# Twelve of 98 edge groups take their source rows from TensorE instead of gathers

## The chip, the cores and the metric

The kernel runs on one core of a Trainium2 chip. The metric is the device time of one execution in microseconds (us), the median of several. A core has TensorE (PE, matrix products into PSUM), VectorE (DVE), ScalarE (ACT), GpSimd (POOL, which issues the gathers here) and SyncE (SP, which issues the other transfers). Each works through its own list of instructions in order and waits on semaphores.

## The reference

One layer of a graph network over N = 6250 nodes and E = 100000 edges, with H = 128 features and 4 attributes per edge. Edges are sorted by destination. All data are float32.

```python
msg_in = concatenate([x[src], x[dst], edge_features], axis=1)
h = silu(msg_in @ mW1 + mb1)
messages = h @ mW2 + mb2
aggregated = segment_sum(messages, dst, num_segments=N)
u = silu(concatenate([x, aggregated], axis=1) @ uW1 + ub1)
out = layer_norm(x + layer_norm(x + u @ uW2 + ub2, ln_g, ln_b))
```

The last line is shortened: the inner norm is that of the layer, and the outer adds the input once more, without gain and bias.

## The kernel before

The first product is split by its rows: A = x @ mW1[:128] and B = x @ mW1[128:256] + mb1 are made once per node and stored in DRAM as tab_a and tab_b. An edge then needs A[src] + B[dst] + (attributes @ the last four rows).

Edges are worked in 98 groups of 1024 (eight tiles of 128 edges; the last group has six). Because edges are sorted by destination, a group touches a window of at most 80 successive nodes. For each group g:

- fetch (L181): POOL issues eight indirect transfers, each of which gathers 128 rows of A for the 128 sources of a tile, into a buffer "ga". There are six such buffers, and fetch runs four groups ahead in program order.
- load: SP brings the destinations (near), the 80 rows of B (mv) and the attributes (st, lower rows), three groups ahead.
- matrices: DVE compares, and so makes the 0/1 matrix st (L468: node by edge, with the count of edges per node) and its turned form oh (L478: edge by node), two groups ahead.
- before_rows (L500): eight products st x mv give B[dst] plus the attributes' part in PSUM (pre), one group ahead.
- hidden: DVE adds pre to the gathered rows (L515), ACT applies silu (L516) and so makes h.
- sums (L524): eight products h x oh, accumulated in PSUM (pt), sum h over the edges of each node. A small product (L522) turns the edge counts.
- add (L545): DVE adds the sums into an accumulator acc at an offset held in a register, and likewise the counts.

The order in which these calls stand in the loop is the order on each engine; there is no other scheduler:

```python
        load(g + LEAD)
        hidden(g)
        matrices(g + 2)
        if g + 1 >= RAW:
            before_rows(g + 1)
        add(g, sums(g))
        node_stage(g)
```

The first five groups (RAW) are gathered from x itself while tab_a is being made. PE turns their rows (L489) and multiplies them by the weights (L502). Nodes are finished in batches of four tiles of 128 nodes, one batch about every eight groups. When a batch closes, node_stage runs node_u in that group (products L562, L569, L570, silu, and the B rows of a later batch by L328), node_y in the next (products, then means and variances on DVE) and node_z in the one after (ACT scales, DVE multiplies, adds, and takes moments). Once at the end a flag (bad_i, from checks) tells whether the destinations fit the windows; if not, a general branch does everything again.

Of the kernel before, what the change touches and what calls it, by code (L numbers as in the profile page):

```python
# [1 line left out]

# [7 lines left out]
I32 = mybir.dt.int32  # L10
BF16 = mybir.dt.bfloat16
AF = mybir.ActivationFunctionType
# [6 lines left out]
P = 128  # L19
# [5 lines left out]
def kernel(  # L25
# [24 lines left out]
    G = 8  # L50
# [27 lines left out]
    assert rest_t == 5 and last[NB - 3] == NG - 10  # L78

    consts = ctx.enter_context(tc.tile_pool(name="consts", bufs=1))  # L80
    dram = ctx.enter_context(tc.tile_pool(name="dram", bufs=1, space=DRAM))
# [15 lines left out]
    edges = ExitStack()  # L97
    edges.enter_context(tc.manual_schedule())
    gath = edges.enter_context(tc.tile_pool(name="gath", bufs=AHEAD + 2))
    work = edges.enter_context(tc.tile_pool(name="edge", bufs=2))  # L100
# [9 lines left out]
    def narrow():  # L110
        return ps1.tile([P, 2 * P], F32, name="pt")

    def bank():
        return ps1.tile([P, BN, P], F32, name="pn")

    src_l = first.tile([SQ, SK, P], I32, name="src_l")
    nf_e = E // P
# [33 lines left out]
    nc.gpsimd.iota(w_row_i, pattern=[[1, W]], base=0, channel_multiplier=0)  # L151
    p_col_i = first.tile([P, 1], I32, name="p_col_i")
    nc.gpsimd.iota(p_col_i, pattern=[[0, 1]], base=0, channel_multiplier=1)

# [16 lines left out]
    tab_a = dram.tile([NP, H], F32, name="tab_a")  # L171
    tab_b = dram.tile([NW, H], F32, name="tab_b")
    ea_d = dram.tile([ED, NG * GE], F32, name="ea_d")
    rows, bases, near = {}, {}, {}
# [13 lines left out]
    for g in range(RAW - 1):  # L188
# [7 lines left out]
        ceil_i, pattern=[[BN * P, NB + 1], [0, G]], base=BN * P - W, channel_multiplier=0  # L196
    )
    fetch(RAW - 1)

# [16 lines left out]
    dst_l = dst_l[:NG]  # L216
    w_row = ps1.tile([P, W], F32, name="w_row")
    nc.vector.tensor_copy(w_row, w_row_i)
    p_col = consts.tile([P, 1], F32, name="p_col")
    nc.vector.tensor_copy(p_col, p_col_i)  # L220
    ones = consts.tile([P, P], F32, name="ones")
# [10 lines left out]
    off_i = consts.tile([1, NG], I32, name="off_i")  # L232
    bad_i = consts.tile([1, 1], I32, name="bad_i")

    def to_row(col, n):
# [4 lines left out]
    def destination_lists():  # L240
        base_c = first.tile([NG, 1], F32, name="base_c")
        nc.vector.tensor_copy(base_c, dst_l[:, 0:1])
        rel_n = first.tile([P, GE], F32, name="rel_n")[:NG]
        nc.vector.tensor_scalar(rel_n, dst_l, base_c, None, op0=OP.subtract)
        pt = wide()
        for i in range(G):
            nc.tensor.transpose(pt[:, i, :NG], rel_n[:, i * P : (i + 1) * P], ident[:NG, :NG])
        nc.vector.tensor_copy(rel.rearrange("c g i -> c i g"), pt[:, :, :NG])
        base_f = first.tile([1, NG], F32, name="base_f")
        row = to_row(base_c, NG)  # L250
        nc.vector.tensor_copy(base_f, row)
        p_b = narrow()
        nc.tensor.matmul(p_b[:, :NG], ones[0:1, :], base_f, start=True, stop=True)
        nc.vector.tensor_scalar(base_p, p_b[:, :NG], p_col, None, op0=OP.add)
        nc.vector.memset(floor_i[:, 0:1], 0)
        nc.vector.memset(floor_i[:, last[NB - 2] + 1 :], batches[NB - 1][0] * P)
        off = first.tile([1, NG], F32, name="off")
        nc.vector.tensor_copy(off, floor_i)
        nc.vector.tensor_sub(off, base_f, off)
        nc.vector.tensor_scalar(off_i, off, 0.0, float(AW - W), op0=OP.max, op1=OP.min)  # L260
        nc.vector.memset(ceil_i[:, 84 + G // 2 :], batches[NB - 1][0] * P - W)
        nc.vector.memset(ceil_i[:, 92 + G // 2 :], NP)
        lim = first.tile([1, NG], F32, name="lim")
        nc.vector.tensor_copy(lim, ceil_i[:, G // 2 : G // 2 + NG])
        nc.vector.tensor_tensor(base_i, base_f, lim, op=OP.min)
        return rel_n, base_f, off, lim

    def checks(rel_n, base_f, off, lim):
        far = first.tile([NG, 2], F32, name="far")
# [5 lines left out]
        nc.vector.tensor_reduce(far[:, 0:1], far, AX.X, OP.max)  # L275
        worst = first.tile([1, 4], F32, name="worst")
        nc.vector.tensor_reduce(worst[:, 0:1], to_row(far[:, 0:1], NG), AX.X, OP.max)
# [62 lines left out]
    def make_a(k, pm):  # L340
        i0, n = batches[k]
        product(k, 0, pm)
        ta = first.tile([P, BN, H], F32, name="ta", bufs=3)
        nc.vector.tensor_copy(ta[:, :n], pm[:, :n])  # L344
        nc.sync.dma_start(by_node(tab_a)[:, i0 : i0 + n, :], ta[:, :n])

# [92 lines left out]
    offs = {}  # L439

    def load_bases(g):
        for to, of, eng, top in ((bases, base_i, ENG.SP, NP), (offs, off_i, ENG.DVE, AW - W)):
# [10 lines left out]
    def load(g):  # L453
        if g >= NG:
            return
        destinations(g)
        if g % RB == 0:
            load_bases(g)
        nc.sync.dma_start(mv[g % NM][:W], tab_b[bass.ds(bases[g], W), :])
        nc.sync.dma_start(stbuf[g % NST][W:], ea_d[:, g * GE : (g + 1) * GE])  # L460

    oh, pre, xg = {}, {}, {}

    def matrices(g):
        if g >= NG:
            return
        n = tiles_of(g)
        nc.vector.tensor_scalar(  # L468
            stbuf[g % NST][:W],
            near.pop(g),  # L470
# [22 lines left out]
    def before_rows(g):  # L493
# [3 lines left out]
        pre[g] = wide()  # L497
        st = stbuf[g % NST].rearrange("k (i c) -> k i c", i=G)
        for i in range(tiles_of(g)):
            nc.tensor.matmul(pre[g][:, i, :], st[:, i, :], mv[g % NM], start=True, stop=not raw)  # L500
            if raw:
                nc.tensor.matmul(  # L502
                    pre[g][:, i, :], xg[g][:, i, :], w1[:, 0, :], start=False, stop=True
                )
        xg.pop(g, None)

    def hidden(g):
        n = tiles_of(g)
        h = hbuf[g % 2]
        p = pre.pop(g)  # L510
# [7 lines left out]
    def sums(g):  # L518
        n = tiles_of(g)
        h, o = hbuf[g % 2], oh.pop(g)  # L520
        pt = narrow()
# [105 lines left out]
    def node_stage(g):  # L627
# [10 lines left out]
        for k in range(2, NB):  # L638
# [4 lines left out]
            if g == G * k - G:  # L643
                make_b(k)

    open_batch(0)
    for g in range(2):
        load(g)
        matrices(g)
    load(2)  # L650
    turned_rows(0)
    for g in range(NG):
        if g == 2:
# [3 lines left out]
        if g == 6:  # L657
            checks(*lists)
            source_lists(1, SK)
            start.close()  # L660
        for c in range(1, NC):
            if g == max(1, c * EC // GE - 8):
                attributes(c)
            if g == max(1, c * EC // GE - 8) + 1:
                attribute_rows(c)
        if g + AHEAD >= RAW:
            fetch(g + AHEAD)
        if g < RAW:
            if g + 1 < RAW:
                turned_rows(g + 1)  # L670
            before_rows(g)
        load(g + LEAD)
        hidden(g)
        matrices(g + 2)
        if g + 1 >= RAW:
            before_rows(g + 1)
        if g == NG - 1:
            node_x(NB - 1)
        add(g, sums(g))
        node_stage(g)  # L680
    k = NB - 1
# [271 lines left out]
```

## Time and profile before

| what | value |
|---|---|
| median of 3 timed executions | 1033.82 us (1021.22 to 1034.26) |
| the profiled execution | 1463.32 us, its span 1461.5 us |
| TensorE's mean granted clock in it | 0.561 of full speed |
| TensorE busy | 885.3 us (61%) |
| VectorE busy | 451.3 us (31%) |
| ScalarE busy | 238.8 us (16%) |
| GpSimd busy | 739.3 us (51%) |
| gathers from tab_a | 742, mean 943 ns |
| gathers from x | 40, mean 947 ns |

In the groups and timelines of the profile a line reads: start in us, busy time in us, engine, source line, operation, what it writes <- what it reads, shape, number of instructions, and in brackets the idle time of the engine just before, with what ended it. In the list of waits a line reads: who waited <- for whom, total us, times, longest. PEclk is the granted TensorE clock in tenths of full speed, in 40 slices of the span. A float32 product of 128x128 by up to 512 columns appears as two MATMUL instructions and two weight loads (PEld). "Remote" stands for a wait whose end the profile can put down to nothing on this core. The profiled execution took longer than the timed ones; the prediction deals with that.

### The profile page before, as it was taken

The page shows a single profiled execution, that of the slowest core. Times are in us where ns is not written, and L with a number is a line of the kernel's source. Part 1 is how long each engine was busy: PE and PEld are TensorE (multiplying, and loading weights), DVE is VectorE, ACT ScalarE, POOL GpSimd, SP SyncE. Part 2 cuts the span into 40 slices and gives each one's busy share as a digit, 9 for nine tenths or more (in the row PEclk, how much of TensorE's full clock was granted, in tenths as well). Part 3 has the DMA queues.
Part 4 walks back from the last instruction along what each step waited for, and adds up shares of the span by engine and source line. Part 5 has one row for each costly group of instructions (what it writes and reads, how often), then busy time and mean ns, then how long its engine had stood idle before and what let it go on. Part 6 is the DMA issues. An engine that isn't in the chain of part 4 may idle for free.

```text
span 1461.5 us, 12138 instructions
## 1 busy us (share of the span) xinstructions
PE 885.3 (61%) x3858; PEld 777.7 (53%) x3858; DVE 451.3 (31%) x936; ACT 238.8 (16%) x338; POOL 739.3 (51%) x792
## 2 busy tenths in 40 slices
PE   2355766466456747554764764766764764764794
PEld 2355755464455645443763663664653763663683
DVE  0032332322322422412522422422422422422443
ACT  0010112111111201201201301211201201201213
POOL 7334555464554654564564565465564565465400
PEclk9987756556555555555555555555555555555555
DMA  6243313122222222221321321331331321322200
GB/s 165 61 117 92 94 58 87 54 83 63 78 79 61 84 68 77 74 77 41 96 84 47 100 81 51 87 92 52 93 92 46 91 86 52 88 65 64 85 26 19
DMA packets 83074, 110.01 MB, mean 75 GB/s; under 512 B 21084, under 2 KB 62160, under 8 KB 83002
## 3 DMA queue, kind: packets, MB, share of 16 engines
q1 hardware_dynamic: 54178, 55.97, 13.2%
q0 software_dynamic: 25024, 51.30, 12.6%
q10 hardware_dynamic: 3800, 1.88, 0.5%
q8 instruction: 33, 0.54, 0.1%
q14 instruction: 39, 0.32, 0.1%
HBM read 97.81 MB, written 11.27 MB: 75 GB/s over the span
## 4 chain that ended last, share of the span: by engine, by line
another core or an unknown queue 37%; PE 25%; DVE 16%; issue 12%; ACT 5%; DVEq 2%; DMA 1%; POOL 1%; ACTq 0%; SPq 0%
PE pt L524 12%; PE pre L500 4%; DVE ga L515 4%; DVE st L468 4%; ACT h L516 3%; DVE oh L478 2%; PE pn L569 2%; PE pn L570 2%; ACT pn L597 2%; DVE bn L556 1%; PE pn L328 1%; DVE var L557 1%; PE pre L328 1%; DVEq L515 1%
## 5 line engine op out<-in xcount | busy, mean ns | idle before, releaser
L181 POOL DMA_INDIRECT ga<-tab_a,src_i x742 | 699.9, 943 | 638.5 <-ACT h L516 372.1
L524 PE MATMUL pt<-oh,h 128*128 128x80 f32 x1564 | 348.1, 415 | 174.6 <-ACT h L516 156.8
L524 PEld LDWEIGHTS pt<-oh,h 128*128 128x128 f32 x1564 | 332.8, 323 | 194.9 <-ACT h L516 172.2
L500 PE MATMUL pre<-mv,st 84*128 84x128 f32 x1564 | 351.0, 409 | 23.1 <-issue 22.1
L500 PEld LDWEIGHTS pre<-mv,st 84*128 84x128 f32 x1564 | 332.4, 318 | 28.3 <-issue 27.0
L545 DVE TENSOR_TENSOR acc<-acc,pt 128x80 f32 x98 | 23.4, 238 | 733.1 <-remote 504.1
L516 ACT ACTIVATE h<-ga 128x1024 f32<-128x1024 f32 (+1 forms) x93 | 98.1, 1055 | 726.2 <-DVE ga L515 541.1
L522 PE MATMUL pt<-ident,deg_g 80*1 80x80 f32 x98 | 30.9, 315 | 191.6 <-DVE deg L545 191.6
L468 DVE TENSOR_SCALAR_CACHE_REDUCE st<-near,base_p 80x1024 f32<-80x1024 int32 x98 | 124.3, 1269 | 7.1 <-issue 5.2
L515 DVE TENSOR_TENSOR ga<-ga,pre 128x1024 f32<-128x1024 f32 (+1 forms) x93 | 113.2, 1217 | 26.8 <-issue 22.0
L522 PEld LDWEIGHTS pt<-ident,deg_g 80*1 80x1 f32 x98 | 10.7, 109 | 199.7 <-DVE deg L545 199.6
L478 DVE TENSOR_TENSOR oh<-w_row,rel 128x640 f32<-128x640 f32 x98 | 79.8, 814 | 0.0
L569 PE MATMUL pn<-acc,wc 128*128 128x512 f32 (+2 forms) x26 | 24.3, 1037 | 89.2 <-DVE acc L545 89.2
L569 PEld LDWEIGHTS pn<-acc,wc 128*128 128x128 f32 x26 | 6.9, 312 | 106.2 <-DVE acc L545 104.1
L181 POOL DMA_INDIRECT ga<-in_x_dram,src_i x40 | 37.9, 947 | 14.2 <-issue 11.7
L321 PE MATMUL pre<-ident,x 128*128 128x128 f32 x49 | 13.8, 434 | 43.6 <-issue 26.6
L321 PEld LDWEIGHTS pre<-ident,x 128*128 128x128 f32 x49 | 8.6, 216 | 47.5 <-issue 26.9
L328 PEld LDWEIGHTS pn<-w,xT 128*128 128x128 f32 x98 | 20.2, 305 | 25.6 <-ACT uT L572 22.7
L597 ACT ACTIVATE pn<-y,r 128x128 f32<-128x128 f32 x49 | 22.6, 461 | 65.6 <-DVE r L590 59.0
L344 DVE COPY ta<-pre 128x512 f32<-128x512 f32 (+2 forms) x13 | 8.6, 661 | 75.9 <-remote 42.3
L337 DVE TENSOR_TENSOR o<-pn,b 128x512 f32<-128x512 f32 (+2 forms) x13 | 8.6, 661 | 74.3 <-PE pn L328 63.1
L536 ACT COPY acc<-acc 128x256 f32<-128x256 f32 (+1 forms) x12 | 5.0, 413 | 159.8 <-DVE acc L545 155.8
(117 smaller groups left out, 532.8 us busy)
## 6 DMA issues: line engine op xcount, KB each, us to landing
near<-in_dst_dram SPq DMA_DIRECT2D x97, 320.0 KB
ga<-tab_a,src_i POOLq DMA_INDIRECT x742
mv<-tab_b SPq DMA_DIRECT2D x98, 40.0 KB
x<-in_x_dram SPq DMA_DIRECT2D x14, 256.0 KB
tab_a<-ta SPq DMA_DIRECT2D x11, 256.0 KB
tab_b<-o SPq DMA_DIRECT2D x11, 256.0 KB
out_dram<-o SPq DMA_DIRECT2D x11, 256.0 KB
st<-ea_d SPq DMA_DIRECT2D x98, 16.0 KB
```

Of the source, the lines that this page charges most:

```text
L181: nc.gpsimd.indirect_dma_start(out=rows[g][:, i, :], out_offset=None, in_=x if g < RAW else tab_a[:, :], in_offset=bass.IndirectOffsetOnAx ...
L328: nc.tensor.matmul(pm[:, i, :], xT[k][:, i * P : (i + 1) * P], w1[:, part, :], start=True, stop=True)
L468: nc.vector.tensor_scalar(stbuf[g % NST][:W], near.pop(g), base_p[:W, g : g + 1], 0.0, op0=OP.is_equal, op1=OP.add, accum_out=deg_g[:, g : ...
L478: nc.vector.tensor_tensor(oh[g][:, :n], w_row[:, None, :].to_broadcast([P, n, W]), rel[:, g, :n, None].to_broadcast([P, n, W]), op=OP.is_e ...
L500: nc.tensor.matmul(pre[g][:, i, :], st[:, i, :], mv[g % NM], start=True, stop=not raw)
L515: nc.vector.tensor_add(s[:, :n], s[:, :n], p[:, :n])
L516: nc.scalar.activation(h[:, :n], s[:, :n], AF.Silu)
L522: nc.tensor.transpose(pt[0:1, P : P + W], deg_g[:, g : g + 1], ident[:W, :W])
L524: nc.tensor.matmul(pt[:, :W], h[:, i, :], o[:, i, :], start=i == 0, stop=i == n - 1)
L569: nc.tensor.matmul(p, wc, acc[k][:, : n * P], start=False, stop=False)
L570: nc.tensor.matmul(p, bc_row, deg[k][:, : n * P], start=False, stop=True)
L597: nc.scalar.activation(to[:, i, :], v[:, i, :], AF.Identity, bias=r[:, 1, lo + i : lo + i + 1], scale=r[:, 0, lo + i : lo + i + 1],)
```

## The change

Groups 12, 19, 26 to 89 (every seventh, twelve in all) are no longer gathered. Their 1024 edges are sorted by source. Since sources are drawn evenly over the nodes, the edges that use a given tile of 128 nodes then lie in a narrow, known range of columns. A is kept in SBUF (49 tiles), a 0/1 matrix O tells which row of a tile an edge takes, and PE multiplies A's tile by that range of O.

- The sort is a bitonic one over 1024 keys (source, destination in the window, tile, place), for all twelve groups at once: 96 partitions of 128 keys. It is 232 small DVE instructions, which stand in the raw groups 0 to 4, between matrices and add. The list of all sources is turned into place in group 0 (in group 6 before). The sorted fields go to DRAM (sd) once.
- A sorted group's work is spread over the six groups before it, d groups ahead: loads of its fields (d = 6), comparisons with the destinations and the tile (d = 5), four sets of 0/1 matrices O, half by comparison on DVE, half by square and relu on ACT (d = 5 to 2), the attributes' part (d = 4, 3), the products with A (d = 3, 2, 1 and 0).
- These products give the transposed sum, feature by edge, in two halves of 512 edges. ACT applies silu, PE turns the result back, ACT copies it, and then sums, add and node_stage run as for any group.
- The other 86 groups keep their path. Their leads now count along a list without the sorted groups (`ahead`, `turn_of`), so gathers, loads and buffers go on as if those were not there.
- PSUM: the bank of pt also holds w_row now (`misc`), and two banks are added (po, px). [...]
- checks also tests that the sorted sources lie within the assumed ranges (`apart`).

```diff
+    Q0, QD, QN = 12, 7, 12
+    by_sort = {Q0 + QD * q: q for q in range(QN)}
+    listed = [g for g in range(NG) if g not in by_sort]
...
-        ta = first.tile([P, BN, H], F32, name="ta", bufs=3)
-        nc.vector.tensor_copy(ta[:, :n], pm[:, :n])
-        nc.sync.dma_start(by_node(tab_a)[:, i0 : i0 + n, :], ta[:, :n])
+        nc.vector.tensor_copy(A[:, i0 : i0 + n], pm[:, :n])
+        nc.sync.dma_start(by_node(tab_a)[:, i0 : i0 + n, :], A[:, i0 : i0 + n])
...
+    def sorted_matrices(g):
+        t = sel[0]
+        nc.vector.tensor_scalar(
+            t["st"][:W], now["ar"][:W], p_col[:W], 0.0,
+            op0=OP.is_equal, op1=OP.add, accum_out=deg_g[:, g : g + 1],
+        )
+        nc.vector.tensor_scalar(t["Oc"], now["sc"][:, 1], p_col, None, op0=OP.is_equal)
+
+    def picks(c):
+        half, r0 = c // 2, c % 2 * (G // 2)
+        O = sel[0]["O"]()
+        key = now["sc"][:, 0, half * HB : (half + 1) * HB]
+        for j in range(G // 2):
+            r = r0 + j
+            if j < 2:
+                nc.vector.tensor_scalar(
+                    O[:, j], key, p_rows[:, r : r + 1], None, op0=OP.is_equal
+                )
+            else:
+                nc.scalar.activation(O[:, j], key, AF.Square, bias=p_less[:, r : r + 1])
+        nc.scalar.activation(O[:, 2:], O[:, 2:], AF.Relu, bias=ones[:, 0:1], scale=-1.0)
+        now[c] = O
...
+    def select(c):
...
+        for i, (b, lo, hi) in enumerate(todo):
+            nc.tensor.matmul(
+                po[:, lo:hi], A[:, b, :], O[:, b % G - r0, lo:hi],
+                start=False, stop=c % 2 == 1 and i == len(todo) - 1,
+            )
...
+    def sorted_before(g):
+        k = next((k for k in by_sort if g < k <= g + 6), None)
+        d = None if k is None else k - g
+        if d == 3:
+            select(0)
+            attribute_part(1)
+        if d == 4:
+            attribute_part(0)
+        if d == 2:
+            select(1)
+            sorted_hidden()
+        if d == 1:
+            turned_hidden(k, 0)
+            select(2)
+        if d == 6:
+            load_sorted(k)
+        if d == 5:
+            sorted_matrices(k)
+        if d in (5, 4, 3, 2):
+            picks(5 - d)
+        if d == 1:
+            sorted_oh(k)
+
+    def sorted_behind(g):
...
+        if d == 4:
+            begin_half(0)
+        if d == 2:
+            begin_half(1)
...
+        if g in by_sort:
+            select(3)
+            sorted_hidden()
+            turned_hidden(g, 1)
+            add(g, sums(g))
+            node_stage(g)
+            continue
...
-        load(g + LEAD)
+        load(ahead(g, LEAD))
         hidden(g)
-        matrices(g + 2)
+        matrices(ahead(g, 2))
+        if g == 0:
+            source_lists(1, SK)
+            todo = sort_steps()
+        if g < RAW:
+            n = -(-len(todo) // (RAW - g))
+            for step in todo[:n]:
+                step()
+            todo = todo[n:]
         if g + 1 >= RAW:
-            before_rows(g + 1)
+            before_rows(ahead(g, 1))
         if g == NG - 1:
             node_x(NB - 1)
+        sorted_before(g)
         add(g, sums(g))
+        sorted_behind(g)
         node_stage(g)
```

Lines of the changed kernel that the prediction names: L987 are the selecting products, L931 the comparison in sorted_matrices. All other line numbers are those of the kernel before.

## The prediction

> **What bounds the kernel now.** I read the page first, then the waits, then two stretches of the timeline: a pair of groups in the steady loop and the close of a batch.
>
> ```profile
> span 1461.5 us, 12138 instructions
> PE 885.3 (61%) x3858; PEld 777.7 (53%) x3858; DVE 451.3 (31%) x936; ACT 238.8 (16%) x338; POOL 739.3 (51%) x792
> PEclk9987756556555555555555555555555555555555
> ...
> DVE acc L545 <- remote: 504.1, 35, 15.5
> POOL ga L181 <- ACT h L516: 372.1, 53, 15.6
> ```
>
> No engine is full, and the clock of TensorE stands at half speed for most of the span. The two waits are one loop: DVE waits 15 us for something that the profile cannot name, h comes late, and POOL waits for a free buffer of rows.
>
> ```profile
> 511.96 0.94 POOL L181 DMA_INDIRECT ga<-tab_a,src_i  x1 [0.30 <-issue]
> 513.21 0.94 POOL L181 DMA_INDIRECT ga<-tab_a,src_i  x1 [0.31 <-issue]
> 517.17 0.24 DVE L545 TENSOR_TENSOR acc<-acc,pt 128x80 f32 x1 [15.46 <-remote]
> 517.70 1.22 DVE L515 TENSOR_TENSOR ga<-ga,pre 128x1024 f32<-128x1024 f32 x1 [0.16 <-issue]
> 519.09 1.06 ACT L516 ACTIVATE h<-ga 128x1024 f32<-128x1024 f32 x1 [18.17 <-DVE ga L515]
> 520.20 3.70 PE L524 MATMUL pt<-oh,h 128*128 128x80 f32 x16 [2.31 <-ACT h L516]
> 520.41 0.94 POOL L181 DMA_INDIRECT ga<-tab_a,src_i  x1 [6.26 <-ACT h L516]
> 523.69 3.70 PE L500 MATMUL pre<-mv,st 84*128 84x128 f32 x16
> 523.93 0.24 DVE L545 TENSOR_TENSOR acc<-acc,pt 128x80 f32 x1 [3.08 <-PE pt L524]
> ```
>
> Every such unnamed wait stands before an instruction that waits for a TensorE result, and ends about 3 us after a burst of gathers (last one issued at 513.21, sum at 517.17). The timed executions cannot hold them: the profiled one took 1463.3 us, the median is 1034. So I set up two limits without them. **POOL:** first gather from tab_a at 93.1, then 742 at 1.247 us (513.21 − 511.96), then 23 us from the last group's L515 (1438.4) to the end: 93 + 925 + 23 = 1041. **The chain of a group** (L515, ACT, L524, L545): 523.93 − 517.17 = 6.76 us, plus the node stage. In the chain of waits a batch adds 7.3 us (u), 5.0 (y) and 6.5 (z), so 18.8 per 8 groups, 2.35 a group: 9.1. It starts at 172.7, some 12 of which are unnamed waits: 160 + 93 x 9.1 + 23 = 1029. POOL's 1041 is 0.7% from the median, so I take the timed kernel to be bound by the issue of gathers, **with the chain only 12 us behind**. Numbers below are in this frame and are brought to the median by 1034/1043 (0.991; 1043 is 1041 and the 1.8 us around the span).
>
> The chain has a second price:
>
> ```profile
> 569.17 2.08 PE L569 MATMUL pn<-acc,wc 128*128 128x512 f32 x2 [9.80 <-DVE acc L545]
> 575.89 2.95 PE L500 MATMUL pre<-mv,st 84*128 84x128 f32 x16
> 579.15 2.01 PE L524 MATMUL pt<-oh,h 128*128 128x80 f32 x16 [0.23 <-ACT h L516]
> 583.13 1.95 PE L500 MATMUL pre<-mv,st 84*128 84x128 f32 x16
> 588.62 3.71 PE L524 MATMUL pt<-oh,h 128*128 128x80 f32 x16 [3.47 <-ACT h L516]
> ```
>
> After dense node products the same sixteen instructions take 2.0 us, and 3.7 again once PE has paused.
>
> [...] L500 and L524 alone do not raise it: at 612 to 626 PE was busy throughout at 0.50. [...]
>
> **The change part by part.**
>
> Gathers: 12 x 8 = 96 fewer, 96 x 1.247 = 120 us off POOL, leaving 646 (806 us).
>
> Sort: 232 small DVE instructions stand between the raw groups 0 to 4, ahead of each group's L545. The nearest rows (98x2 and 1x98, each dependent on the one before) start every 0.2 us: 46 us; bounds 35 (0.15, as L545's two follow each other) and 60. The raw phase ran from 112.8 to about 160; DVE's own work there is 5 x 3.9 = 19 us, and the source lists moved there are 3. 46 + 19 + 3 = 68, and some 2 us per group of waiting for PE and ACT: 78. So the loop starts at 190, not 160. POOL cannot run past it: its six buffers are full and group 11 needs h of group 5.
>
> TensorE per sorted group: 672/12 = 56 selecting products, mean width 117, plus four products 512 wide (px, po) and 8 transposes; 8 of L500 go. At full clock a product costs 0.222 to 0.235 us (L500 with L502 at 134 to 137: two instructions per 0.22; L524 2.01 for eight with its drain), a 512 one about 0.95: 13.2 + 3.8 + 1.8 − 1.8 = 17 us. At half clock (0.45, 2.07): 25.2 + 8.3 + 3.5 − 3.5 = 33.5 us.
>
> DVE per sorted group: L931 1.27, Oc and eight O. Their price is bounded by rel_n (L244, 98x1024 in 0.75 us) and L468 (1.27): Oc 1.0, O 0.5 each, px parts 2 x 0.65, oh_s 0.8: 8.4, against 3.3 saved. Beside PE, except five groups ahead, where DVE has 7.1 us in a row. ACT gains 8 squares, 4 Relu and 4 copies, 11 us over four groups of 7 us or more: hidden behind PE's products; uncovered it would add 2.3 to a group. SP's six extra transfers go out a whole group ahead of their use; nothing urgent is behind them.
>
> **The chain of one block of seven**, PE at full clock. Six groups ahead: 4.9 (2.5 for L515 and ACT, 1.95 L524, 0.5). Five: 7.1 (DVE). Four: 6 (px and po on PE). Three: L500 1.9 + select 3.8 + px 0.9 + L524 1.95 = 8.6. Two: 1.9 + 2.9 + 1.95 + po 0.9 = 7.7. One: 1.9 + transposes 0.9 + 3.05 + 1.95 = 7.8. The sorted group itself: select 3.5, silu 0.7, transposes 0.9, copy 0.7, half of its sums 0.95: 6.8. Together 48.9. Node stage: u falls to 4.2 (223.1 to 226.9), so 15.7 x 7/8 = 13.7, of which selections fill about 3 that PE spent idle: 10.7. Block: 59.6, against 7 x 9.97 = 69.8 before and POOL's 59.9 after.
>
> Total: 190 + 12 x 59.6 + 9 groups outside the blocks x 9.1 + 23 = 1010, x 0.991 = **1000 us**. Every microsecond of a block is worth 12.
>
> **Rivals.**
> (a) The clock does not hold. What decides is PE's pause between blocks and in the groups six to four ahead, which have only L500 and L524. If selections begin cold, [...] three ahead 11, four ahead 9.5, six ahead 6.8, others as above: 56 + node stage 11 = 67, giving 190 + 804 + 82 + 23 = 1099, x 0.991 = 1089. This ends slower: from a block of 64.1 us (1055) on. For it: the half clock in 35 of 40 slices. Against it: selections are 128 deep and mostly wider than 100, like the raw groups' products, which raised the clock within 4 us at 113. Wholly cold a block is about 95 (1435); the raw groups speak against that.
> (b) POOL stays the bound: node stage and selections overlap better than I count. POOL restarts at 191 with 75 groups: 191 + 75 x 9.97 + 23 = 962, x 0.991 = 953.
> (c) The sort costs twice what I think in the head (60 us): 1030, no difference.
> (d) The check on the sorted order sends the kernel through its general branch. From the inputs the distance stays at 16 against the allowed 400, so no.
>
> **How the numbers follow.** Forecast 1000 us (block 56 to 61: 960 to 1015): 0.38. (a) 0.36, (b) 0.12, (c) and what is between 0.14. The range takes (b) with a cheaper sort (945) and (a) up to 67.5 us a block (1095). Faster by over 2% (about what a measurement of this kernel can tell from no change): most of the forecast and all of (b), 0.46. Within 2%: rest of the forecast, (c), the light end of (a): 0.19. Slower: 0.35.
>
> **What would show it.** In the profile after: about 686 gathers and 648 us of POOL; L987's 1344 instructions with a mean near 275 ns, as L502's median (421, L524's median: rival a); PEclk above 7 in most slices from a quarter on; group 5's L515 some 30 us later; the wait for h before L181 small in timed runs, which the profile, with its unnamed waits, cannot show directly. I am wrong if L987 runs at half clock in most groups, if ACT or DVE holds PE before a selection, or if gathers slow down beside the DVE comparisons.

## The result: slower by 5%

The changed kernel takes 1077.44 us (median of 4, 1076.21 to 1080.96) against 1027.52 us before (median of 4): ratio 1.0494, 95% interval 1.0393 to 1.0594. The forecast was 1000 us. Ratios use each kernel's executions within 1.5% of its fastest, while the profiled executions of a_wrow_c, a_noprod_b and g12_c are slower than that, up to 1.1% above the kernel's median.

In four of the seven sets of runs below, the kernel before takes 1453 to 1476 us, and in the other three 1025 to 1028. The first are called long sets, the others short, and a ratio is always one against the kernel before in the same set. The result belongs with the short sets, and so does the profile of the changed kernel: it took 1080.96 us and holds none of the unnamed waits. The changed kernel itself was not measured again in a short set, so where its ratio is compared with that of another run, the difference is good to some 11 to 15 us.

### The profile after

Three lines of the page:

```profile
span 1079.2 us, 15122 instructions
...
PE 864.4 (80%) x5206; PEld 764.1 (71%) x5206; DVE 556.2 (52%) x1321; ACT 368.2 (34%) x518; POOL 658.4 (61%) x697
...
PEclk9966765787987968869679698888879879698565
```

TensorE is busy for 80% of the span now and its clock stands mostly at 6 to 9 tenths, as the prediction hoped. POOL's gathers are fewer by 96. Neither made the kernel faster. The list of waits tells what POOL does instead:

```profile
DVE acc L601 <- PE misc L580: 240.7, 88, 9.3
...
POOL ga L213 <- issue: 196.6, 637, 2.8
POOL ga L213 <- ACT h L572: 125.8, 24, 28.6
PEld misc L578 <- DVE oh L534: 123.4, 51, 8.5
PE misc L578 <- DVE oh L534: 106.4, 41, 8.3
```

"Issue" (637 times 0.31 us) is POOL's normal step from one gather to the next. The next POOL line is time lost: 125.8 us of waiting until ACT has read a buffer of rows (h), more than the 120 us that 96 gathers less save. So the chain through h sets the pace. The last two lines name a wait that the prediction does not have: L578, the small product that begins each group's sums, waits for L534, the 0/1 matrix of the group two ahead. Before, L522 waited for L545 only (PE 191.6 us, 24 times).

The timeline of one ordinary group shows it (start us, duration us, engine, line):

```profile
583.75 1.22 DVE L571 TENSOR_TENSOR ga<-ga,pre 128x1024 f32<-128x1024 f32 x1 [0.15 <-issue]
...
584.89 1.27 DVE L524 TENSOR_SCALAR_CACHE_REDUCE st<-near,base_p 80x1024 f32<-80x1024 int32 x1
585.00 1.06 ACT L572 ACTIVATE h<-ga 128x1024 f32<-128x1024 f32 x1 [0.76 <-DVE ga L571]
...
586.08 0.82 DVE L534 TENSOR_TENSOR oh<-misc,rel 128x640 f32<-128x640 f32 x1
...
586.96 0.23 PE L578 MATMUL misc<-ident,deg_g 80*1 80x80 f32 x1 [1.55 <-DVE oh L534]
...
587.02 2.07 PE L580 MATMUL misc<-oh,h 128*128 128x80 f32 x16
...
589.13 0.24 DVE L601 TENSOR_TENSOR acc<-acc,misc 128x80 f32 x1 [2.23 <-PE misc L580]
```

ACT begins h at 585.00 and is done at 586.06. The sums could begin then. They begin at 586.96, just after DVE has finished the comparison L534 at 586.90. The reason is the PSUM tile `misc`: the change puts w_row, which L534 reads, into the tile of pt, which L578 writes. The two use different columns, and still the writer waits for the reader: 41 times on PE and 51 on its weight loads, as the list shows. The trace doesn't tell whether the wait follows the bank or the tile, since w_row and pt are slices of one tile here. In this group it costs 0.9 us, on the chain through h.

The groups of the page that the prediction named:

```profile
L580 PE MATMUL misc<-oh,h 128*128 128x80 f32 x1372 | 238.1, 347 | 5.0 <-ACT h L572 5.0
L556 PE MATMUL pre<-mv,st 84*128 84x128 f32 x1372 | 232.7, 334 | 10.4 <-DVE xg L547 10.4
...
L987 PE MATMUL po<-O,A 128*128 128x157 f32 (+47 forms) x1344 | 172.3, 287 | 0.0
```

L987's mean is 287 ns (275 forecast, 421 if cold): the selections run warm. They take 172.3 us, 14.4 for each sorted group. L580 and L556, the products of the ordinary groups, have means of 347 and 334 ns, against 415 and 409 in the profile before: some groups are warm (sixteen instructions in 1.95 us) and some cold (3.62 to 3.70). One place where they are cold is where a batch closes (TensorE alone):

```profile
594.25 1.16 PE L382 MATMUL pn<-w,xT 128*128 128x128 f32 x8 [0.78 <-ACT uT L628]
595.25 3.35 PE L556 MATMUL pre<-mv,st 84*128 84x128 f32 x16
599.25 0.29 PE L578 MATMUL misc<-ident,deg_g 80*1 80x80 f32 x1 [0.66 <-DVE oh L534]
599.34 3.62 PE L580 MATMUL misc<-oh,h 128*128 128x80 f32 x16
602.89 2.07 PE L634 MATMUL pn<-ub_row,ones 1*128 1x512 f32 x2
...
606.76 3.11 PE L556 MATMUL pre<-mv,st 84*128 84x128 f32 x16
```

In the group of the node products and in the one after, sixteen instructions take 3.1 to 3.6 us again. The granted clock is 0.61 from 590 to 610 us, and 1.00 from 640 to 660, in a block's selections. The other place is the quiet groups six to four ahead of a sorted one, which have no selections: groups 20 and 21 take 3.62 and 3.70 us for their sixteens, at a clock of 0.53 (318 to 341 us).

### The profile page after: what moved, and what is told of

The parts are those of the page before. It is cut to its first block, busy times and chain, and to the rows that moved or that the text cites. A ratio compares the mean times of both kernels' runs of the same rounds, so it can differ in the third digit from the quotient of the medians.

```text
span 1079.2 us, 15122 instructions
## 1 busy us (share of the span) xinstructions
PE 864.4 (80%) x5206; PEld 764.1 (71%) x5206; DVE 556.2 (52%) x1321; ACT 368.2 (34%) x518; POOL 658.4 (61%) x697
## 5 line engine op out<-in xcount | busy, mean ns | idle before, releaser
L213 POOL DMA_INDIRECT ga<-tab_a,src_i x646 | 618.9, 958 | 339.7 <-issue 184.8
L580 PE MATMUL misc<-oh,h 128*128 128x80 f32 x1372 | 238.1, 347 | 5.0 <-ACT h L572 5.0
L556 PE MATMUL pre<-mv,st 84*128 84x128 f32 x1372 | 232.7, 334 | 10.4 <-DVE xg L547 10.4
L580 PEld LDWEIGHTS misc<-oh,h 128*128 128x128 f32 x1372 | 229.4, 261 | 16.4 <-issue 10.4
L556 PEld LDWEIGHTS pre<-mv,st 84*128 84x128 f32 x1372 | 221.5, 248 | 21.1 <-DVE xg L547 10.6
L572 ACT ACTIVATE h<-ga 128x1024 f32<-128x1024 f32 (+1 forms) x81 | 85.4, 1055 | 317.9 <-DVE ga L571 207.2
L987 PE MATMUL po<-O,A 128*128 128x157 f32 (+47 forms) x1344 | 172.3, 287 | 0.0
L987 PEld LDWEIGHTS po<-O,A 128*128 128x128 f32 x1344 | 171.0, 198 | 0.0
L601 DVE TENSOR_TENSOR acc<-acc,misc 128x80 f32 x98 | 23.3, 238 | 241.0 <-PE misc L580 240.7
L578 PE MATMUL misc<-ident,deg_g 80*1 80x80 f32 x98 | 25.9, 264 | 116.2 <-DVE oh L534 106.4
L524 DVE TENSOR_SCALAR_CACHE_REDUCE st<-near,base_p 80x1024 f32<-80x1024 int32 x86 | 109.1, 1269 | 7.1 <-DMA near<-in_dst_dram 7.1
L571 DVE TENSOR_TENSOR ga<-ga,pre 128x1024 f32<-128x1024 f32 (+1 forms) x81 | 98.4, 1215 | 27.1 <-DMA ga<-tab_a,src_i 18.1
L578 PEld LDWEIGHTS misc<-ident,deg_g 80*1 80x1 f32 x98 | 8.6, 87 | 137.3 <-DVE oh L534 123.4
L953 ACT ACTIVATE O<-sc,p_less 128x512 f32<-128x512 f16 x96 | 63.5, 709 | 37.1 <-PE po L987 37.1
L534 DVE TENSOR_TENSOR oh<-misc,rel 128x640 f32<-128x640 f32 x86 | 70.0, 814 | 0.4 <-ACT bc_row L484 0.4
L954 ACT ACTIVATE O<-O,ones 128x1024 f32<-128x1024 f32 x48 | 55.1, 1148 | 1.6
L949 DVE TENSOR_SCALAR O<-sc,p_rows 128x512 f32<-128x512 f16 x96 | 44.7, 506 | 5.3 <-PE po L987 3.7
L391 DVE TENSOR_TENSOR o<-pn,b 128x512 f32<-128x512 f32 (+2 forms) x13 | 8.6, 661 | 57.7 <-PE pn L382 57.6
```

Of the source, the lines that this page charges most:

```text
L213: nc.gpsimd.indirect_dma_start(out=rows[g][:, i, :], out_offset=None, in_=x if g < RAW else tab_a[:, :], in_offset=bass.IndirectOffsetOnAx ...
L524: nc.vector.tensor_scalar(stbuf[turn_of(g) % NST][:W], near.pop(g), base_p[:W, g : g + 1], 0.0, op0=OP.is_equal, op1=OP.add, accum_out=deg ...
L534: nc.vector.tensor_tensor(oh[g][:, :n], w_row[:, None, :].to_broadcast([P, n, W]), rel[:, g, :n, None].to_broadcast([P, n, W]), op=OP.is_e ...
L556: nc.tensor.matmul(pre[g][:, i, :], st[:, i, :], mv[turn_of(g) % NM], start=True, stop=not raw)
L571: nc.vector.tensor_add(s[:, :n], s[:, :n], p[:, :n])
L572: nc.scalar.activation(h[:, :n], s[:, :n], AF.Silu)
```

## The experiments

Two accounts are used. The first is POOL's, read off the timeline: first gather from tab_a, 1.249 us for each further one, what it stalled beyond that (waits, and gathers that took longer), and what follows the start of the last gather. All rows are from short sets.

| profiled kernel | first gather | gathers x 1.249 | stalls | after the last | span |
|---|---|---|---|---|---|
| after | 57.7 | 805.6 | 149.2 | 66.7 | 1079.2 |
| w_row in SBUF (a_wrow_c) | 55.2 | 805.6 | 104.5 | 63.4 | 1028.7 |
| no sort (a_nosort_b) | 55.4 | 805.6 | 104.9 | 65.9 | 1031.9 |
| both (a_wn) | 55.2 | 805.6 | 57.8 | 63.0 | 981.7 |
| no selecting products (a_noprod_b) | 59.2 | 805.6 | 102.0 | 60.9 | 1027.7 |
| w_row in SBUF, fp16 selections (a_f16w_b) | 60.5 | 805.6 | 90.9 | 30.0 | 987.1 |
| before, shared bank (b_wait_b) | 59.0 | 925.5 | 19.4 | 61.8 | 1065.7 |
| before, 96 gathers left out (g12_c) | 58.4 | 805.6 | 79.5 | 64.1 | 1007.6 |

The second is the prediction's own: when group 5's sums are added (the head), the mean time of a block of seven groups from there to group 89, and the rest.

| profiled kernel | group 5 added at | block of seven | after group 89 |
|---|---|---|---|
| after | 169.4 | 68.0 | 94.0 |
| a_wrow_c | 156.4 | 65.2 | 90.3 |
| a_nosort_b | 119.0 | 68.3 | 93.2 |
| a_wn | 120.2 | 64.3 | 90.4 |
| a_noprod_b | 169.8 | 63.7 | 94.0 |
| a_f16w_b | 171.1 | 60.2 | 93.6 |
| b_wait_b | 127.4 | 69.8 | 101.1 |
| g12_c | 124.8 | 65.9 | 92.5 |

My theory after the result was: the shared bank costs 50 to 70 us and the sort in the head 25 to 40. The rivals were the work of the selecting products, and a clock that falls in the node stage.

### The shared bank

```diff
-    w_row = misc[:, 2 * P : 2 * P + W]
+    w_row = consts.tile([P, W], F32, name="w_row")
```

In long sets:

> The changed kernel with w_row, the row of numbers that oh is compared with, in a tile of its own in SBUF instead of in the PSUM bank that pt shares. In the changed kernel the small product L578 at the head of a group's sums waits for L534 (oh of the group two ahead) on DVE, since both touch misc; in the kernel before it waited for the add of the previous group. L534 ends 3.15 us after L571 starts, h is ready after 2.3: 0.85 us a group. Theory C (this wait is in the chain): some 60 to 86 groups x 0.85 = 50 to 70 us less, 1077 falls to 1007 to 1027. Rival (PE has no time to spare there anyway): under 15 us, 1062 or more. If the comparison, now with two inputs from SBUF, held up gathers, POOL's mean per gather would rise above 0.96 us and the time with it.

> The changed kernel with w_row in SBUF, so that the bank misc is pt's alone. Theory shared bank (each ordinary group's L578 waits for L534, 0.85 us x about 75 groups): 50 to 70 us less than the changed kernel, 0.98 to 1.0 of the kernel before. Theory TensorE at half clock or too much product work: at most 20 us less, 1.03 or higher.

Measured: 0.9688 (0.960 to 0.9775) and 0.967 (0.957 to 0.977), where the changed kernel itself stands at 0.986 (below): some 27 us less, and not the 50 to 70 expected. In a short set:

> The changed kernel with w_row in SBUF, sorting kept, once more. Theory that the two losses add up, the bank being the larger (0.85 us x about 75 groups): 60 of the 95 us, so 0.99 of the kernel before where that takes about 1027 us. Theory that the sort in the head is the larger: at most 35 us, 1.015 or higher. Where the kernel before takes about 1450 us: 0.967, as before.

Measured: 0.994 (0.9907 to 0.9972). Against the changed kernel's 1.0494 that is 57 us of some 1026, by one line. L534 itself takes as long as before (0.815 us), so it is the wait that went: of the waits of L578 for L534, 123.4 us on the weight loads, 2.6 are left, and POOL's wait for h falls from 125.8 us to this (waits of a_wrow_c):

```profile
POOL ga L213 <- ACT h L572: 70.1, 15, 31.1
```

The block falls from 68.0 to 65.2 us, 34 us in twelve, and the head by 13: between 85 and 170 us of the changed kernel L578 waits 14.8 us in three groups for L534, which stands behind sort steps. The first theory's size held, its working did not: 0.85 us in each of some 75 groups would be 64 us in the loop, where the twelve blocks gave 34.

The edit has a price, which the expectation had named. With w_row in SBUF the mean of a gather rises to 997 ns (958 in the changed kernel, 943 in the kernel before). One of the longest, beside the DVE comparisons (a_wrow_c):

```profile
801.20 1.74 POOL L213 DMA_INDIRECT ga<-tab_a,src_i  x1 [0.30 <-issue]
...
801.31 0.82 DVE L534 TENSOR_TENSOR oh<-w_row,rel 128x640 f32<-128x640 f32 x1
...
802.04 0.81 DVE L1009 TENSOR_TENSOR oh_s<-w_row,rel_s 128x640 f32<-128x640 f32 x1
```

The gather ends at 802.94, just after L1009 at 802.85, and the next begins 2.05 us after it, not 1.25. In this run 79 gathers take more than 1.1 us (31 us over 0.943 in all), in the changed kernel 31 (8 us), in the kernel before and b_wait_b none from tab_a. Of the gathers with L534 beside them 50 of 126 are that long, against 9 of 98 in the changed kernel, where L534 reads w_row from PSUM; with no DVE instruction beside them none is. So the bank cost at least what this run gained. In how far the held gathers lie on the path here was not tried.

### The sort

```diff
-        return todo + [spread, distance]
+        return [make, spread, distance]
```

(and the threshold of the check on the order so that it never fires). In a long set and in a short one:

> The changed kernel without the stages of the sort: the keys go unsorted to the twelve groups (so their products pick wrong rows), and the test on the order is neutralised. About 210 of 232 small DVE instructions go. Theory D (the sort lies open in the head): POOL waited 28.6 us for h of group 5 and the raw groups took 12 to 19 us each; without the sort 25 to 40 us less, 1037 to 1052. Rival (the chain later makes up for it, since six groups of rows are then ready): under 10 us.

> The changed kernel without its sort stages (the sorted groups' part of the output is left out), the bank still shared, once more. Theory bank larger: 35 of the 95 us go, 1.015 of the kernel before where that takes about 1027 us. Theory sort larger: 60 us or more, 0.99 or lower. Where the kernel before takes about 1450 us: 0.964, as before.

Measured: 0.9637 (0.956 to 0.971) and 1.0145 (1.005 to 1.024). In the short set that is 36 us less than the changed kernel (47 between the two profiled executions). It is all in the head: group 5 is added at 119.0 and not 169.4, while a block stays at 68. What the sort's stages cost is seen in DVE's timeline of the changed kernel, one raw group:

```profile
100.44 0.24 DVE L601 TENSOR_TENSOR acc<-acc,misc 128x80 f32 x1
...
103.81 0.19 DVE L807 TENSOR_TENSOR key<-key,po 96x32 f32<-96x32 f32 x1
104.04 0.21 DVE L807 TENSOR_TENSOR po<-key,po 96x32 f32<-96x32 f32 x1
...
116.25 0.21 DVE L807 TENSOR_TENSOR po<-key,po 96x32 f32<-96x32 f32 x1
116.37 0.24 DVE L601 TENSOR_TENSOR acc<-acc,misc 128x80 f32 x1
```

The two L601 are those of groups 0 and 1. Between them lie 12.6 us of sort steps, each started 0.22 us after the last, and group 1's addition, whose sums PE had finished at 107.65, stands behind them.

Both edits together:

> The changed kernel with w_row in SBUF and without its sort stages (the keys stay in the order of the list, so the sorted groups' part of the output is left out). Theory that the shared bank and the sort in the head explain the loss: both savings add up, 80 to 100 us less than the changed kernel, 0.95 to 0.97 of the kernel before where that takes about 1027 us; where it takes about 1450 us, 0.986 - 0.019 - 0.022 = 0.945. Theory that one of them hides the other (the head ends where the first wait is): no more than the better of the two alone, 0.96 to 0.97 there. Theory product work: 1.03 where the kernel before takes 1027 us.

Measured: 0.9606 (0.9505 to 0.9708), 982.88 us, by the ratios 91 us less than the changed kernel. 57 and 36 add up; the stalls of the first table say the same (149.2, less 45 and 44, gives 60; measured 57.8). The waits of this kernel:

```profile
...
PEld misc L580 <- ACT h L572: 97.5, 37, 7.7
...
POOL ga L213 <- ACT h L572: 29.7, 9, 9.3
```

POOL's wait for h is down to 29.7 us, and the sums wait for h (L572), not for L534. So these two account for the whole loss of 5%, and for a gain of 4% that they had covered.

### The selecting products

```diff
-        for i, (b, lo, hi) in enumerate(todo):
-            nc.tensor.matmul(
-                po[:, lo:hi], A[:, b, :], O[:, b % G - r0, lo:hi],
-                start=False, stop=c % 2 == 1 and i == len(todo) - 1,
-            )
```

> The changed kernel without its selecting products (L987): the 12 sorted groups get only the first addend of their rows, so that part of the output is left out; sorting, O and the shared bank stay. Theory TensorE-bound (a block's time is the sum of its groups' TensorE steps): the products and the wait for them go, 1344 x 0.287 / 2 = 193 us of half-width pairs less what lies in TensorE's gaps; at least 100 us less than the changed kernel, so 0.95 of the kernel before or lower. Theory gather-bound: POOL has 650 gathers x 1.247 + 93 = 904 us as floor, so between 0.90 and 0.93. Theory that the shared bank and the sort cause the loss: at most 40 us less than the changed kernel, 1.01 of the kernel before or higher.

> The changed kernel without its selecting products (the sorted groups' rows are left out of the output), bank shared and keys sorted, once more. Theory that a block is bound by TensorE: 12 x 16 us of products less 2 us of gaps, so 1077 - 100 or more, 0.95 or lower where the kernel before takes about 1027 us. Theory that a block is bound by the chain through h and the products fill its gaps: 30 us or less, 1.02 or higher. Where it takes about 1450 us: 0.95, as before.

Measured: 0.950 (0.9425 to 0.957) in the long set and 0.9892 (0.984 to 0.9947) in the short one, 62 us less than the changed kernel by the ratios and 52 between the profiled executions. The page counts 172.3 us of L987, so about a third of it was on the path: the expectation of 100 us or more fails, and so does the one of 30 or less. The block is 63.7 us: 14.4 us of products gone, 4.3 gained. Without them the clock falls too (0.697 as against 0.782 mean), and L556 and L580 are busy for 38 us more in all, so the run may understate the products.

Cheaper products instead of none: A as a high and a low fp16 part (two products each, accumulated in float32; as a float32 product appears as two instructions, their number stays 1344), O in fp16, w_row in SBUF. The core of the edit:

```diff
-                po[:, lo:hi], A[:, b, :], O[:, b % G - r0, lo:hi],
-                start=False, stop=c % 2 == 1 and i == len(todo) - 1,
+                po[:, lo:hi], A[:, s, b, :], O[:, b % G - r0, lo:hi],
+                start=False, stop=c % 2 == 1 and i == len(todo) - 1 and s == 1,
```

> The changed kernel with A kept as a high and a low fp16 part, O in fp16, two products of each selection in place of one float32 product, and w_row in SBUF. Theory product work: two fp16 products of 128 x 128 take about half of one float32 one (0.287 us), so some 1344 x 0.07 = 90 us of TensorE go, of which about 60 lie on the path: with the bank, 110 to 130 us less than the changed kernel, 0.93 to 0.95. Theory shared bank alone: as the run with w_row in SBUF.

> The changed kernel with w_row in SBUF, A as two fp16 parts, O in fp16 and two fp16 products for each float32 one, once more. Theory that TensorE's products are on the path: 0.994 (w_row in SBUF alone) less 40 us or more, 0.955 or lower. Theory that they fill gaps: 0.98 or higher. Where the kernel before takes about 1450 us: 0.97.

Measured: in the long set a median of 1421.96 us against 1457.17, with runs from 1372 to 1435, too spread to tell; in the short set 0.9529 (0.943 to 0.963), 984.91 us. From the float32 form with w_row in SBUF (0.994) that is 42 us. Page and waits of the short run:

```profile
span 987.1 us, 15164 instructions
...
PEclk9997675596596795967959879989759769597575
...
L993 PE MATMUL po<-O,A 128*128 128x157 f16 (+47 forms) x1344 | 82.2, 219 | 0.0
```

```profile
...
POOL ga L213 <- ACT h L575: 46.2, 5, 31.0
```

Selections take 82.2 us for 172.3, so two fp16 products took 0.48 of a float32 one, the half that the expectation had. POOL waits for h five times, 31.0 us of it once, in the head. A block takes 60.2 us, and 48 gathers at 1.249 are 60.0: this kernel has reached the gathers' pace, and what follows the last gather falls to 30 us, which fits a chain that no longer lags by full buffers. It beats both kernels. Its head is 15 us longer than that of a_wrow_c (the edit also splits A there), and the comparisons that make O on DVE are shorter (0.35 us for 0.49, 14 us in all), so the 42 us are not the products' alone. Of its gathers, 65 are held beyond 1.1 us, 27 us in the loop; where POOL sets the pace, these should count in full, but no run without them was made.

### What bounds the kernel before

> The kernel before with one edit: w_row lies in the bank of pt, as the change puts it, and nothing is sorted. Theory shared bank (every group's L578-like product waits for the selection of two groups ahead, 0.85 us x 87 groups): 50 to 75 us more than the kernel before where that takes about 1027 us (ratio 1.05 to 1.07); where it takes about 1450 us, 20 to 75 us more (1.015 to 1.05). Theory product work: no difference within 1% (0.99 to 1.01).

> The kernel before with w_row in the bank of pt and nothing else, once more. Theory that the kernel before is bound by the chain through h as the changed kernel is: 85 groups x 0.7 us, 1.05 or more where the kernel before takes about 1027 us. Theory that it is bound by the issue of gathers, the chain being 12 us behind (the prediction's frame): 1.03 to 1.04. Theory that its chain has a lot of slack: within 1%. Where it takes about 1450 us: 1.0, as before.

```diff
+    misc = ps1.tile([P, 4 * P], F32, name="misc")
-        return ps1.tile([P, 2 * P], F32, name="pt")
+        return misc[:, : 2 * P]
-    w_row = ps1.tile([P, W], F32, name="w_row")
+    w_row = misc[:, 2 * P : 2 * P + W]
```

Measured: 1.0013 (0.9975 to 1.005) in a long set, where longer waits cover it; 1.0313 (1.021 to 1.042) in a short one, 32 us. The waits of the short run (two lines are added ahead, so L524 is L522 of before and L480 is L478):

```profile
...
ACT h L518 <- DMA ga<-tab_a,src_i: 209.6, 33, 12.5
PEld misc L524 <- DVE oh L480: 164.8, 80, 10.2
...
POOL ga L183 <- ACT h L518: 22.6, 9, 7.4
```

The same wait is there (164.8 us on PE's loads), yet POOL waits for h for 22.6 us only, almost all before 200 us: the block is 69.8 us, which is 56 x 1.249 = 69.9, and ACT waits 209.6 us for rows. So even with the extra wait the steady loop goes at the gathers' pace, and the kernel before cannot be slower there. The 32 us must lie in the head and after the last gather. How they are split stays open, as no profile of the kernel before came from a short set. The head up to group 5 can have little of it: g12_c, which is the kernel before up to there, adds group 5 at 124.8, and this run at 127.4.

> The kernel before with the gathers of groups 12, 19 to 89 left out and nothing in their place (those groups take silu of pre alone, so their rows of A are missing from the sums). It is the gain of the change without its cost: 96 gathers x 1.25 us = 120 us less of POOL. Theory A, gathers pace the kernel and the chain is only some 12 us behind: 1027 falls to about 1000 to 1010. If gathers paced it alone with the chain far behind: about 910. Theory B, the chain already paces it: the twelve groups lose only L515, 12 x 1.3 = 15 us, so about 1010 to 1020.

> The kernel before without the gathers of the 12 groups (those groups' part of the output is left out) and nothing in their place. Theory gather-bound (96 x 1.247 = 120 us): 0.885 to 0.90 of the kernel before where that takes about 1027 us. Theory of the prediction's frame (chain 12 us behind the gathers): the chain takes over at once, 0.98 to 0.99. Where it takes about 1450 us: 0.924, as before.

```diff
-        if g >= NG:
+        if g >= NG or g in LEFT:
...
-        if g < RAW:
+        if g < RAW or g in LEFT:
```

Measured: 0.9237 (0.916 to 0.931) in the long set and 0.9678 (0.955 to 0.981) in the short one: 33 us (20 to 46), not 120. Its waits in the short set:

```profile
...
PEld pt L526 <- ACT h L518: 96.6, 30, 9.3
...
POOL ga L183 <- ACT h L518: 82.5, 23, 7.2
```

Now POOL waits for h (82.5 us). A block takes 65.9 us, against 60.0 for its 48 gathers: the chain takes over. So 96 gathers fewer are worth some 33 us as long as the chain through h stays as it is: more than the 12 of the prediction's frame, and far less than 120.

### The kernels themselves once more

> The kernel before, unchanged, profiled once more. If the 35 unnamed waits before L545 (504 us in all) belong to that one profiled execution, this one shows a span near 1025 to 1035 us, and its steady loop tells what paces it. Theory A (gathers pace it): POOL issues a gather every 1.25 us without a break and waits for h less than 30 us in all after the first groups. Theory B (the chain of a group paces it): POOL waits for h again and again, 100 us or more in all. If the waits belong to the program, the span is again about 1460.

> The changed kernel itself, unaltered, as the measure for the other runs of this set: 1.049 of the kernel before where that takes about 1027 us. Where the kernel before takes about 1450 us, the theory that results of TensorE are held back there until a burst of gathers is over expects less than 1.0, since the changed kernel issues 96 gathers fewer, in shorter bursts; the theory that the loss is TensorE's own work alone expects 1.0 or more there too (1450 + 50 us).

> The kernel before, unaltered, for its profile in the same set of runs. Theory that it is bound by the issue of gathers: POOL waits almost only for issue (above 90% of its idle time), and a block of seven groups takes 7 x 8 x 1.247 = 69.8 us. Theory that the chain through h bounds it: POOL waits for h more than 50 us, and a block is longer. With the unnamed waits (about 1450 us) it says nothing on that.

All three fell into long sets. The kernel before took 1448.32 and 1457.32 us. Its waits (first of the two):

```profile
ACT h L516 <- DVE ga L515: 544.3, 53, 21.3
DVE acc L545 <- remote: 501.7, 34, 15.5
POOL ga L181 <- ACT h L516: 362.1, 53, 14.6
```

These are the lines of the profile that the prediction read, and here the executions without a profile take as long as the profiled one. The changed kernel took 1430.41 us, ratio 0.9864 (0.977 to 0.995): where these waits exist, the change gains a little. Its list:

```profile
POOL ga L213 <- ACT h L572: 450.3, 53, 28.5
...
DVE acc L601 <- remote: 121.1, 12, 12.2
```

The last run puts the twelve groups seven later, so that the sort is spread over twelve groups, with w_row in SBUF and fp16 selections:

```diff
-    Q0, QD, QN = 12, 7, 12
+    Q0, QD, QN = 19, 7, 12
-        if g == 6:
+        if g == 13:
             checks(*lists, apart)
-        if g < RAW:
-            n = -(-len(todo) // (RAW - g))
+        if g < 12:
+            n = -(-len(todo) // (12 - g))
```

> The changed kernel with w_row in SBUF and fp16 selections, and with the sorted groups put seven later (first 19, last 96), so that the sort's stages are spread over the first twelve groups and not over the five raw ones. Theory that the stages cost time only as they stand in the raw groups, where VectorE has no free time: 25 to 35 us less than with w_row and fp16 alone, 0.92 to 0.93 of the kernel before where that takes about 1027 us. Theory that 232 dependent VectorE instructions cost the same anywhere: 0.95 or higher.

Measured: 0.938 (0.926 to 0.951), 1369.1 us, in a long set. The same kernel with the sort in the raw groups had 1421.96 of 1457.17 in another long set, 0.976 by the medians. But both spread by several per cent, their profiled executions took the same time (1370.3 and 1370.7 us), and in a short set it was not tried. What the place of the stages is worth stays open.

## Why the prediction was wrong, by its steps

Two steps failed: the term for what a block holds beyond its warm groups was too small, and the shared bank, which cost most, had no term at all.

- **The frame.** "The timed executions cannot hold" the unnamed waits: true of the runs of the result, not in general, as the long sets show. The sum for the kernel before (93 + 925 + 23 = 1041) came out near 1028 by two errors that in part cancel. In short sets the first gather from tab_a comes at 55 to 61 us and not at 93, a figure from a profile with the unnamed waits. Of a span of some 1026 us, 925 for gathers and 58 for the start then leave an estimated 43 for stalls and what follows the last gather together, where the sum had 23. What carried the argument, that the steady loop is bound by gathers with the chain close behind, is right: 69.8 us a block by POOL, and 65.9 by the chain (g12_c) where 7 x 9.1 = 64 was forecast.
- **Gathers, 120 us off POOL.** Right in number and in the usual step (1.249 us before and after), and worth 33 us to the kernel. Of the signs of being wrong, "gathers slow down beside the DVE comparisons" did come, at a small price: 31 gathers, 8 us.
- **Sort, the loop 30 us later.** Steps start every 0.22 us, against 0.2 counted: 51 us for 232. But the head grew by 50 us (119.0 to 169.4): none of the steps fell into idle time, as some were counted to. In the time it is 36 to 47 us. The sign named for it was group 5's L571 thirty us later: it starts at 159.6, and at 109.7 without the sort. The sum had it at 190 and 160, figures that rest on a profile with the unnamed waits, so the loop starts 30 us earlier than forecast for all that. That these two errors go opposite ways is luck.
- **TensorE per sorted group.** Right: 14.4 us of selections against 13.2, at full clock (1.00 from 640 to 660 us).
- **The warm block, 48.9 us.** Right as a sum of best cases: taking for each place in the block the fastest of its twelve groups, a_wrow_c gives 4.9 + 6.2 + 5.2 + 9.2 + 6.5 + 8.0 + 6.8 = 46.8. The changed kernel gives 50.4, since the bank holds the quiet groups.
- **The term that failed: "node stage 10.7, block 59.6".** A mean block is 68.0 us in the changed kernel, 65.2 without the shared bank. In a_wrow_c, compare each group with the fastest at its place in the block, as above: 18.4 us of a mean block lie beyond those. Of these, 13.9 are in the groups of a closing batch (u, y and z: 5.6, 3.5 and 4.8). The prediction had 13.7 there and took off 3, which "selections fill"; the net shows nothing of that. The other 4.5 are in groups without node products (1.2 of them in groups 6 and 8, still under the head), which the prediction had at full clock throughout. But groups 20 and 21 take 7.04 us each, with TensorE busy from 297 to 311 us without a gap at a granted clock of 0.50, and groups 13 to 15 take 4.94, 6.25 and 5.17, at 0.96 (239 to 256). Against the forecast that is 3.2 and 4.5 more, less 2.1 by which the warm groups are shorter: 5.6 us a block, 67 us in twelve. How the closing batch's share divides between clock and order was not isolated: no experiment changes the clock alone.
- **The term that was missing.** That w_row moves into pt's bank stood in the diff; the wait of L578 for L534 that comes with it in the trace (106.4 us on PE) had no cost in the prediction. Measured: 57 us by a_wrow_c, most of the 77 us by which the forecast missed. Between the profiles it is 34 us in the blocks (2.8 each), 13 in the head and 4 after group 89.
- **The sum, put together.** Twelve blocks of 68.0 for 59.6 are 101 us more; group 5 is added at 169.4 and not at 199 (190 + 9.1), 30 less; the rest is 94.0 for 95.8, 2 less: 1010 becomes 1079. The factor 0.991, which fitted the sum for the kernel before to its median, took another 9 off the forecast.
- **Rival (a)** named a block of 67 us and 1089 us. Its 11 and 9.5 us for the groups three and four ahead were the author's estimate of a cold start; the profile before shows one such start in the raw groups, about 4 us at 0.50 (113 to 117 us). The numbers came near (68.0, 1077), in good part by luck: the selections, which it had cold, were warm, and 2.8 us of the block are the bank's. Its cold groups ahead of the selections did occur, in some of the blocks. Rival (b), POOL as the bound, is what a_f16w_b became.

## What to carry to other kernels

When a tile moves into a bank or buffer that another one uses, list who reads and who writes either of them, and draw the new wait on the chain of the loop before pricing anything else: here one line of allocation cost about as much as the sort (57 us, the sort 36 to 47). Removing work from the engine that is the bound is worth only the distance to the next bound, which a run with that work simply left out measures at once (33 of 120 us). Small dependent instructions in a head can cost their whole sum (here 50 us for 51), since everything behind them in the queue waits with them (group 1's addition, whose sums were ready at 107.65, began at 116.37). And a tile moved between PSUM and SBUF changes what else is held: here 79 gathers took more than 1.1 us, for 31 before the move.

## What the runs showed of the hardware

In four of seven sets DVE waits up to 15.5 us before L545 of the kernel before, 34 or 35 times, about 500 us in all. Mostly the last product that it waits for had ended 11 to 12 us before by the profile, ten gathers were issued during the wait, and DVE went on 3.9 us after the start of the last of them. As the profile models the ends of products, the traces don't tell whether TensorE finished late or DVE learned of it late. In the other three sets the kernels show no such wait. What differs between the sets is not known from these runs. It is not the chip alone: the chip numbered 5 gave one long set and two short ones. TensorE itself is stretched there in one place (in the profile before, the sixteen L500 from 592.12 on lasted until 598.8 with gaps that nothing explains), and the cost of the same edit changes with it: 3% for the shared bank in one kind of set, 0.1% in the other.

Gathers from tab_a last 0.943 us on POOL, at most 0.96 in the kernel before. Beside some DVE comparisons whose inputs all lie in SBUF they can last until those end, up to 1.8 us in a_wrow_c: beside L534 there, and in the changed kernel mostly beside L949, which makes O (24 of the 31 long ones). This reading rests on what runs side by side in the traces, and on the one edit that moved w_row.
